# Gated feed-forward with a ternary down projection on one core: the buffers of down_w's late parts, and a new order of the first batch's steps

## The chip, the core and the metric

The kernel runs on one core of a Trainium2 chip. The core has a matrix engine (PE, with a weight-load queue PEld beside it), a vector engine (DVE), a scalar engine (ACT), a general engine (POOL) and a sync engine (SP), which issues nearly all transfers of this kernel (DMA). Each engine takes its instructions strictly in the order of the program; engines wait for each other by semaphores. The metric is the device time of one execution in microseconds (us), lower is better; several executions give a median.

## What is computed

`x` is (4, 1024, 512), `cond` is (4, 128), `norm_w` (512, 128), `up_w` (4096, 512), `down_w` (512, 2048), all float32. Cut to what matters:

```python
scale = cond @ norm_w.T + 1.0
ms = mean(x * x, axis=-1)
h = x * scale * rsqrt(ms + 1e-6)
val, gate = split(h @ up_w.T)            # 2048 columns each
h = val * gelu(gate)
hq = act_quant(h)                        # per token: round(h * 127 / max|h|), scaled back
wq = weight_quant(down_w)                # round(w / mean|w|) clipped to -1, 0, 1, scaled back
y = hq @ wq.T + x
```

## The kernel before

**Blocks and batches.** The four batches of 1024 tokens are taken one after the other. The 4096 rows of `up_w` make 16 blocks of 128 value rows and 128 gate rows; block number g is 16 times the batch plus j. A product in float32 quality is made of float16 halves: a high part and the rest ("low"). Blocks 0 to 11 of the first batch are plain products (`plain`, L715, 12 matmuls each, named `gate.j.h` and `value.j.h` for token half h). From block 12 on a block is made of seven products of six matmuls each by a Strassen-like scheme (`product`, L700): `first`, `fourth`, `second`, then `third` of the block before, `fifth`, `gate` of the block before, `value`. The sums are kept in PSUM banks A (two), B (one), E (two). Between the products stand copies and activations: ACT copies A to B (`first_copy`, L807), E out (`fourth_copy`, L815), A out (`fifth_copy`, L822) and makes the GELUs (`second_gelu`, L829, and `gate_gelu`, L846); DVE makes the outputs (`third_out` L835, `gate_sum` L843, `value_sum` L852, `value_out` L855). `second` adds into B and needs `first_copy`; `value` adds into A and needs `fifth_copy` to have read it; `third` adds into A and needs `value_sum`.

**The first batch** also has to make everything that the other batches use: it scales `up_w` by powers of two, splits and turns it (`w_*`, `rows_*`, `s_sum`, `s_high`, `s_low`, `s_turn`) and spills the parts to DRAM (`s_spill`, L469). It makes the second batch's tokens: for each quarter a of the tokens it loads, scales, sums and splits them (`t_load` to `t_low`) into a buffer with the tag `nx`, and turns that by a transposing transfer in three parts (`t_turn.a.part`, L675; part 0 holds the operands of `first` and `second`, part 1 the operand of `gate`, part 2 the rest). For a = 0 and 2 the tokens themselves stand in the tag `xn`, for a = 1 and 3 in the tag `am`; the four sums of a quarter stand in the tag `xt`. Each of these tags has one buffer. Last, it takes the running maxima (`max.i.h`, L906 and L908).

**down_w** is read twice. The first reading (`d_load`, `d_sum`) gives the mean. The second is done in eight pieces n of 128 x 1024 float32 (512 KB): `d_fetch(n)` (L546) brings a piece into a buffer, `d_round(n)` (L550, ACT) and `d_sign(n)` (L557, ACT) make it ternary in `tn`, and `d_turn(m)` (L560) turns two pieces at once into `wd`. The buffers of the pieces are those of the tokens, used again, by tag; piece 2 has a place of its own in H. A fetch waits until the last reader of its buffer is done, and holds the sync engine while it waits.

**Order.** The whole program's order is written by hand (`manual_schedule`). For the first batch it is a list of 619 steps, `FIRST_BATCH`, found by a search; a step emits its instructions for whichever engines they need. A third number 1 at a `s_sum`, `s_low` or `t_sum` puts that step on DVE, otherwise it is on POOL. The list reaches to the products of block 15. From block 16 on a loop over slots emits the products; there pieces 2 to 7 are rounded by a table (`D_LATE`: `d_round` 2 and `d_sign` 2 in the x part of slot 16, `d_round` 3 in its y part), and `d_turn` 0 and `d_fetch` 4 are issued after slot 16 between the first two loads of block 18's weights (L485, L483).

Of the kernel before, what the change touches and what calls it, by code (L numbers as in the profile page):

```python
# [51 lines left out]
def glu_quant_kernel(  # L52
# [456 lines left out]
    def d_at(n):  # L509

        return n // 4 + 2 * (n % 2), n // 2 % 2, n % 2
# [26 lines left out]
    def d_fetch(n):  # L538

        if n == 2:  # L540
            v = H[:, NJ].rearrange("p h t -> p (h t)")
        else:
            tag = ("xn", "xt", None, "nx", "xn", "xt", "nx", "xn")[n]
            v = wpool.tile([P, HF], F32, name=f"dn_{n}", tag=tag, bufs=1)
        c, u, _ = d_at(n)
        SP.dma_start(out=v, in_=down_w[c * P : (c + 1) * P, u * HF : (u + 1) * HF])  # L546
        dn[n] = v
# [701 lines left out]
    def second_part():  # L1249
# [110 lines left out]
    def take(steps):  # L1360
# [17 lines left out]
        value.3.0 rows_high.5 o_low.3 t_square.0.0 gelu.3.0 rows_low.5 rows_turn.5 o_high.2 gate.3.1 out.2.1
        gelu.3.1 c_range out.3.0 w_load.9 value.3.1 s_spill.4.1 s_sum.3.0.1 s_sum.3.2 w_load.7 w_range.6
        s_spill.3.1 w_load.11 d_load.1 t_square.0.1 s_spill.2.0 w_factor.6 c_spread o_low.2 w_scale.6.1  # L1380
        c_rows gate.4.0 w_scale.6.0 s_sum.3.1.1 s_high.2.1 rows_high.6 s_low.2.1.1 out.3.1 s_sum.3.3
        rows_low.6 rows_turn.6 s_high.3.1 value.4.0 s_high.3.0 s_low.3.0 max.0.0.0 d_sum.3 w_range.7
        max.1.0.0 gate.4.1 t_root.0 o_high.0 c_copy c_store w_factor.7 s_sum.4.1 w_load.8 w_scale.7.0
        o_low.0 gelu.4.0 value.4.1 w_scale.7.1 s_sum.4.0.1 s_sum.4.2.1 rows_high.7 out.4.0 max.1.0.1 d_sum.0
        s_low.3.1.1 gate.5.0 rows_low.7 rows_turn.7 s_high.4.0 s_low.4.0 max.0.1.0 d_sum.1 c_undo gelu.4.1
        value.5.0 out.4.1 w_range.8 c_load s_spill.3.0 s_sum.4.3 d_total s_spill.6.1 s_spill.5.1 w_factor.8
        s_high.4.1 s_low.4.1 w_scale.8.1 max.1.1.0 d_spread gate.5.1 w_scale.8.0 s_sum.5.1 s_sum.5.0.1
        rows_high.8 s_spill.7.1 s_sum.5.2.1 s_spill.2.2 rows_low.8 s_sum.5.3 s_high.5.0 value.5.1
        rows_turn.8 w_range.9 s_low.5.0.1 s_sum.6.0.1 w_factor.9 w_scale.9.0 s_sum.6.2 gate.6.0 c_bring
        w_scale.9.1 t_scale.0.1 w_gain.6 max.1.1.1 gelu.5.1 s_spill.4.0 t_sum.0.0.1 s_spill.4.2 rows_high.9  # L1390
        d_mean value.6.0 out.5.1 s_spill.3.2 s_high.5.1 t_load.1 rows_low.9 t_high.0.1 t_scale.0.0 t_sum.0.2
        w_range.10 gate.6.1 gelu.6.0 w_factor.10 w_gain.8 s_low.5.1.1 s_sum.6.3 s_sum.6.1.1 s_high.6.0
        value.6.1 rows_turn.9 t_sum.0.3.1 gelu.5.0 t_sum.0.1 s_high.6.1 s_low.6.0.1 s_sum.7.0 t_high.0.2
        out.5.0 gelu.6.1 gate.7.0 t_low.0.2 t_high.0.0 w_scale.10.1 s_sum.7.2 w_scale.10.0 s_spill.8.1
        s_sum.7.1.1 t_turn.0.2 rows_high.10 value.7.0 out.6.1 t_low.0.1 gelu.7.0 rows_low.10 s_high.7.0
        s_spill.5.0 s_low.6.1.1 gate.7.1 s_sum.7.3.1 w_range.11 t_low.0.0 t_turn.0.0 out.7.0 t_square.1.0
        w_factor.11 w_scale.11.1 s_low.7.0.1 s_sum.8.1 s_spill.5.2 value.7.1 t_turn.0.1 w_scale.11.0 out.6.0
        t_square.1.1 max.2.0.0 s_spill.6.2 gelu.7.1 t_root.1 rows_turn.10 rows_high.11 gate.8.0 s_sum.8.0.1
        s_high.7.1 s_low.7.1.1 gelu.8.0 s_sum.8.2.1 out.7.1 s_spill.7.2 s_sum.8.3 rows_low.11 s_spill.6.0
        value.8.0 s_spill.9.1 s_high.8.0 s_low.8.0.1 s_spill.8.0 s_high.8.1 gate.8.1 s_sum.9.0.1 out.8.0  # L1400
        s_sum.9.2.1 s_sum.9.1.1 s_high.9.0 s_low.9.0 s_low.8.1.1 s_spill.8.2 s_sum.9.3.1 max.2.0.1 gelu.8.1
        value.8.1 w_load.12 rows_turn.11 max.3.0.0 w_gain.10 w_range.12 t_scale.1.1 gate.9.0 out.8.1
        t_scale.1.0 t_sum.1.1 s_sum.10.0.1 gelu.9.0 t_load.2 s_spill.7.0 t_sum.1.0 t_sum.1.2.1 value.9.0
        s_spill.11.1 s_high.9.1 w_factor.12 t_sum.1.3 w_gain.12 w_scale.12.1 s_sum.10.1.1 s_sum.10.2.1
        t_high.1.2 s_low.9.1.1 s_sum.10.3 gate.9.1 out.9.0 s_spill.10.1 t_high.1.0 s_spill.9.0 s_high.10.0
        w_load.13 t_low.1.2 s_low.10.0.1 value.9.1 t_turn.1.2 s_high.10.1 w_scale.12.0 t_high.1.1
        s_sum.11.1.1 gelu.9.1 s_sum.11.0 rows_high.12 gate.10.0 t_low.1.0 t_turn.1.0 t_square.2.0
        rows_low.12 t_square.2.1 out.9.1 w_range.13 rows_turn.12 s_sum.11.2.1 value.10.0 t_low.1.1
        s_low.10.1.1 gelu.10.0 max.3.0.1 s_high.11.0 t_turn.1.1 s_sum.11.3 s_low.11.0.1 w_load.14 gate.10.1
        s_spill.12.1 t_root.2 w_factor.13 w_scale.13.1 out.10.0 s_high.11.1 s_sum.12.1 s_low.11.1.1  # L1410
        w_scale.13.0 rows_high.13 value.10.1 s_sum.12.0.1 s_sum.12.2.1 rows_low.13 s_high.12.0 s_sum.12.3.1
# [417 lines left out]
```

## Time and profile before

| what | us |
|---|---|
| median of 3 runs | 721.25 (720.65 to 723.73) |
| the profiled execution, own time | 722.66 |
| its span, first to last instruction | 720.8 |
| products of block 16 begin (first, on PE) | 176.35 |
| `d_fetch` 0 and 1 issued | 163.95, 165.82 |
| `d_fetch` 2 and 3 issued | 175.54, 183.22 |

The difference between the profiled execution's own time and its span, 1.86 us, lies outside the first and the last instruction. The page's busy shares are averages over the whole span; what a change in one stage is worth is read from that stage's rows: what each engine waited for, and for how long.

### The profile page before, as it was taken

What the parts mean: (1) busy time and instruction counts of PE and PEld (TensorE: products, weight loads), DVE (VectorE), ACT (ScalarE), POOL (GpSimd) and SP (SyncE); (2) the same over time, 40 slices, a digit from 0 to 9 for tenths busy, and PEclk for the clock granted to TensorE, in tenths of its full rate; (3) what the DMA queues carried; (4) which work ended last, traced back from release to release, by engine and by line L of the source; (5) the groups of instructions that cost most, each with busy time, mean ns of one, the idle gap of its engine ahead of it and who ended that gap; (6) DMA issues with size and microseconds to landing.
All of it is one profiled execution on the core that took longest, in us unless ns stands there. A gap on an engine that the chain in (4) does not pass through costs nothing.

```text
span 720.8 us, 10222 instructions
## 1 busy us (share of the span) xinstructions
PE 712.9 (99%) x3664; PEld 359.6 (50%) x3664; DVE 589.5 (82%) x880; ACT 423.2 (59%) x703; POOL 134.7 (19%) x143
## 2 busy tenths in 40 slices
PE   8999999999899999999999999999999999999998
PEld 4544444444344446665444445665444444445854
DVE  8898898889798879897788867876689888755896
ACT  6998877676568774554335676544433665333473
POOL 1812323240100125340100031460020000000120
PEclk9999999999999999999999999999999999999999
DMA  6899889999976566777644547775944444443253
GB/s 227 282 265 285 256 222 268 243 218 221 247 181 131 132 161 146 196 185 164 156 101 115 131 101 193 175 169 165 208 103 103 101 102 103 99 91 105 104 161 132
DMA packets 227060, 121.57 MB, mean 169 GB/s; under 512 B 188969, under 2 KB 198461, under 8 KB 227010
## 3 DMA queue, kind: packets, MB, share of 16 engines
q1 hardware_dynamic: 226858, 120.80, 67.4%
q8 instruction: 28, 0.46, 0.3%
q14 instruction: 22, 0.18, 0.1%
q10 hardware_dynamic: 152, 0.13, 0.1%
HBM read 52.71 MB, written 23.09 MB: 105 GB/s over the span
## 4 chain that ended last, share of the span: by engine, by line
PE 97%; DMA 1%; ACT 1%; issue 1%; DVE 0%; SPq 0%; DVEq 0%
PE A L700 36%; PE E L700 18%; PE po L1064 9%; PE B L700 9%; PE pg L715 8%; PE pv L715 8%; PE po_end L1016 4%; DMA R<-nx 1%; PE pz L1181 1%; PE ptx L1165 1%; PE pv L786 0%; PE po_B L1064 0%; PE pg L786 0%; PE pw L382 0%; PE po_A L1064 0%
## 5 line engine op out<-in xcount | busy, mean ns | idle before, releaser
L700 PEld LDWEIGHTS <-SXY 128*128 128x128 f16 x2100 | 205.5, 98 | 242.4 <-issue 2.0
L700 PE MATMUL A<-R,SXY 128*128 128x512 f16 x1146 | 264.8, 379 | 0.0
L700 PE MATMUL E<-R,SXY 128*128 128x512 f16 x582 | 141.4, 379 | 0.0
L835 DVE SCALAR_TENSOR_TENSOR H<-A,sg,t 128x512 f32<-128x512 f32 x52 | 38.9, 748 | 66.9 <-PE A L700 66.7
L987 DVE TENSOR_TENSOR H<-H,am 128x1024 f32<-128x1024 f32 x64 | 76.0, 1213 | 0.0
L700 PE MATMUL B<-R,SXY 128*128 128x512 f16 x300 | 72.9, 379 | 1.7 <-ACT B L807 1.7
L846 ACT ACTIVATE t<-t,sg 128x512 f32<-128x512 f32 x52 | 37.4, 720 | 61.8 <-DVE t L843 61.7
L906 DVE TENSOR_REDUCE gm<-H 128x512 f32<-128x1024 f32 x56 | 69.0, 1232 | 1.0
L922 POOL PARTITION_ALL_REDUCE am<-R x8 | 14.3, 1793 | 233.4 <-DVE R L908 233.4
L829 ACT ACTIVATE t<-B,sg 128x512 f32<-128x512 f32 x52 | 35.7, 687 | 37.2 <-PE B L700 37.1
L715 PEld LDWEIGHTS <-SXY 128*128 128x128 f16 x342 | 33.4, 98 | 40.3 <-DVE SXY L424 0.4
L822 ACT COPY t<-A 128x512 f32<-128x512 f32 x52 | 30.2, 581 | 38.0 <-PE A L700 37.5
L1064 PE MATMUL po<-wd,R 128*128 128x256 fp8e4 x416 | 52.4, 273 | 0.0
L815 ACT COPY v<-E 128x512 f32<-128x512 f32 x52 | 30.4, 586 | 32.2 <-PE E L700 30.0
L855 DVE SCALAR_TENSOR_TENSOR H<-v,sg,t 128x512 f32<-128x512 f32 x52 | 41.3, 794 | 9.7 <-ACT t L846 9.6
L1064 PEld LDWEIGHTS <-R 128*128 128x128 bf16 (+1 forms) x448 | 43.8, 98 | 8.9
L807 ACT COPY B<-A 128x512 f32<-128x512 f32 x52 | 29.7, 572 | 31.5 <-PE A L700 30.7
L852 DVE TENSOR_TENSOR v<-A,v 128x512 f32<-128x512 f32 x52 | 35.6, 685 | 9.7 <-PE A L700 8.6
L995 ACT ACTIVATE H<-H 128x1024 f32<-128x1024 f32 x38 | 39.9, 1050 | 5.2 <-DVE H L987 5.2
L908 DVE TENSOR_TENSOR R<-R,gm 128x512 f32<-128x512 f32 x56 | 40.5, 723 | 1.1
L715 PE MATMUL pg<-R,SXY 128*128 128x512 f16 x180 | 41.3, 379 | 0.0
L999 ACT ACTIVATE R<-H 128x1024 bf16<-128x1024 f32 x38 | 40.1, 1056 | 1.0
(237 smaller groups left out, 947.6 us busy)
## 6 DMA issues: line engine op xcount, KB each, us to landing
SXY<-s_dram SPq DMA_DIRECT2D x46, 256.0 KB, 3.1
H<-in_L_cond_up_w_dram SPq DMA_DIRECT2D x13, 512.0 KB, 4.3
SXY<-s_dram SPq DMA_DIRECT2D x46, 128.0 KB, 3.2
s_dram<-SXY SPq DMA_DIRECT2D x15, 384.0 KB, 5.0
xr<-in_x_dram SPq DMA_DIRECT2D x19, 256.0 KB, 2.9
out_dram<-xr SPq DMA_DIRECT2D x19, 256.0 KB, 2.5
H<-in_x_dram SPq DMA_DIRECT2D x8, 512.0 KB, 7.4
R<-in_L_cond_down_w_dram SPq DMA_DIRECT2D x8, 512.0 KB, 6.9
```

The lines of the kernel that those rows point to most:

```text
L700: PE.matmul(o, s[:, w, k, :], operand(g // NJ, c, l, k), start=start and n == 0, stop=stop and n == len(TERMS) - 1, skip_group_check=True,)
L715: PE.matmul(ps, a[k // 2][:, w, k % 2, :], XP[:, l, k, h * TOK : (h + 1) * TOK], start=n == 0, stop=n == len(terms) - 1,)
L829: ACT.activation(self.t1, self.B, AF.Gelu, scale=gain(self.g, 1))
L835: DVE.scalar_tensor_tensor(h_half(self.g, 0), self.A, gain(self.g, 0), self.t1, ALU.mult, ALU.mult)
L846: ACT.activation(self.t2, self.t2, AF.Gelu, scale=gain(self.g, 1))
L855: DVE.scalar_tensor_tensor(h_half(self.g, 1), self.v, gain(self.g, 0), self.t2, ALU.mult, ALU.mult)
L906: DVE.tensor_reduce(gm[0], v, AX.X, ALU.max, apply_absolute_value=True)
L908: return [largest, lambda: DVE.tensor_tensor(m, m, gm[0], ALU.max)]
L987: DVE.tensor_tensor(v, v, r.to_broadcast([P, 2, TOK]), ALU.mult)
L995: ACT.activation(v, v, AF.Copy, bias=MAGIC)
L999: ACT.activation(q, by_tile(v), AF.Copy, bias=-MAGIC)
L1064: PE.matmul(po, w[:, j], m, start=start and j == 0, stop=stop and j == n - 1, skip_group_check=True,)
```

## The change

Two things. First, `d_fetch` gives pieces 3 to 7 other tags: `xn` and `nx` change places, so that piece 3 takes the buffer of piece 0 (`xn`) and piece 4 the one that `t_turn` reads (`nx`). Pieces 4 to 7 follow: 6 takes that of 3, 7 that of 4.

```diff
-            tag = ("xn", "xt", None, "nx", "xn", "xt", "nx", "xn")[n]
+            tag = ("xn", "xt", None, "xn", "nx", "xt", "xn", "nx")[n]
```

Second, the 619 steps of `FIRST_BATCH` stand in another order. Both lists hold the same steps on the same blocks; a few sums move between POOL and DVE (`s_low.14.1`, `s_sum.15.3`, for instance, go to POOL, `s_low.15.0` and two of `t_sum.3` to DVE). The order of PE's instructions does not change at all. The end of the list, cut to the steps that the prediction speaks of:

```diff
-        s_high.15.0 s_low.15.0 t_low.2.1 max.4.0.0 t_high.3.2 slot.14.6 t_high.3.0 slot.12.15 s_spill.15.0
...
-        slot.15.7 d_round.1 s_spill.13.1 max.4.1.1 slot.15.4 d_fetch.2 gains s_spill.15.2 max.5.1.0
-        d_round.0 s_spill.9.2 slot.14.10 slot.15.5 slot.14.9 d_sign.0 max.5.1.1 slot.15.13 slot.14.11
-        t_high.3.1 slot.14.12 slot.15.14 d_sign.1 t_low.3.1 t_turn.3.1 slot.14.15 max.6.0.0 d_fetch.3
-        max.6.0.1 max.6.1.0 s_spill.15.1 s_spill.10.2 s_spill.14.1 max.6.1.1
+        slot.12.15 slot.14.3 slot.13.8 s_low.15.0.1 w_gain.15 t_low.3.2 s_turn.15.0 slot.14.4 slot.14.5
+        slot.13.9 d_fetch.1 slot.13.10 s_spill.15.0 max.4.0.1 d_fetch.0 slot.14.7 max.5.0.0 s_high.15.1
...
+        slot.14.9 t_turn.3.2 d_round.0 slot.15.4 d_sign.0 s_spill.9.2 max.4.1.1 d_fetch.2 slot.14.10
+        max.5.1.0 s_spill.15.2 slot.15.5 s_spill.11.2 s_spill.10.2 slot.15.3 d_fetch.3 slot.15.13 d_sign.1
+        max.5.1.1 s_spill.14.1 s_spill.13.1 slot.14.11 s_spill.15.1 max.6.0.0 slot.14.12 t_high.3.1
+        max.6.0.1 slot.14.15 slot.15.14 max.6.1.0 max.6.1.1 t_low.3.1 t_turn.3.1
```

On the sync engine, where the first two pieces are fetched (`s_rows` to `SXY` is `s_turn`, `s_dram` is written by `s_spill`, `R` from `nx` is `t_turn`: 8x128 is part 0, 16x128 part 2, 4x128 part 1). Before:

```order
L475 DMA_TRANSPOSE SXY_81<-s_rows_15_0_1674 128x8x128
L546 DMA dn_0_1710<-in_L0_cond_down_w_dram 128x1024
L675 DMA_TRANSPOSE R_78<-nx_1_0_963 128x4x128
L546 DMA dn_1_1722<-in_L0_cond_down_w_dram 128x1024
L475 DMA_TRANSPOSE SXY_81<-s_rows_15_1_1675 128x8x128
```

And now:

```order
L475 DMA_TRANSPOSE SXY_81<-s_rows_15_0_1651 128x8x128
L546 DMA dn_1_1714<-in_L0_cond_down_w_dram 128x1024
L469 DMA s_dram_84<-s_rows_15_0_1651 128x1024
L546 DMA dn_0_1724<-in_L0_cond_down_w_dram 128x1024
L475 DMA_TRANSPOSE SXY_81<-s_rows_15_1_1652 128x8x128
```

Piece 1 is fetched ahead of piece 0, and a spill of 256 KB stands between the two.

On the same engine, a little later, from the fetch of piece 2 (into H) to block 18's first load (L485). Before:

```order
L546 DMA H_79<-in_L0_cond_down_w_dram 128x1024
L469 DMA s_dram_84<-s_rows_15_1_1675 128x1024
L469 DMA s_dram_84<-R_78 128x512
L675 DMA_TRANSPOSE R_78<-nx_1_0_963 128x4x128
L546 DMA dn_3_1825<-in_L0_cond_down_w_dram 128x1024
L469 DMA s_dram_84<-SXY_81 128x1536
L469 DMA s_dram_84<-R_78 128x512
L469 DMA s_dram_84<-R_78 128x1536
L485 DMA SXY_81<-s_dram_84 128x1024
```

And now:

```order
L546 DMA H_79<-in_L0_cond_down_w_dram 128x1024
L469 DMA s_dram_84<-s_rows_15_1_1652 128x1024
L469 DMA s_dram_84<-R_78 128x512 x2
L546 DMA dn_3_1808<-in_L0_cond_down_w_dram 128x1024
L469 DMA s_dram_84<-R_78 128x1536
L469 DMA s_dram_84<-SXY_81 128x1536 x2
L675 DMA_TRANSPOSE R_78<-nx_1_0_956 128x4x128
L485 DMA SXY_81<-s_dram_84 128x1024
```

The last turn of the tokens goes from ahead of piece 3's fetch to the end of the list, and the spill of 384 KB from block 13's place in `SXY` (`s_spill.13.1`), which stood ahead of piece 2, goes behind piece 3.

On ACT, around the rounding of pieces 0 and 1 (`B_15` is written by `first_copy`, `t1_15` by `second_gelu`, `t2_15` from A by `fifth_copy`, `v_15` by `fourth_copy`; `t2_14` by `gate_gelu`). Before:

```order
L807 COPY B_15_1746<-A_15_1736 128x512
L815 COPY v_15_1759<-E_15_1751 128x512
L829 ACTIVATE t1_15_1778<-B_15_1746,sg_0_104 128x512
L550 ACTIVATE dn_1_1722<-dn_1_1722,wsc_106 128x1024
L550 ACTIVATE dn_0_1710<-dn_0_1710,wsc_106 128x1024
L822 COPY t2_15_1803<-A_15_1736 128x512
L557 ACTIVATE tn_0_1806<-dn_0_1710,unmagic_74 128x1024
L667 CAST nx_1_0_963<-xa_1_3_1494 128x256
L846 ACTIVATE t2_14_1708<-t2_14_1708,sg_0_104 128x512
L557 ACTIVATE tn_0_1806<-dn_1_1722,unmagic_74 128x1024
```

And now:

```order
L807 COPY B_15_1749<-A_15_1740 128x512
L550 ACTIVATE dn_1_1714<-dn_1_1714,wsc_106 128x1024
L829 ACTIVATE t1_15_1769<-B_15_1749,sg_0_104 128x512
L550 ACTIVATE dn_0_1724<-dn_0_1724,wsc_106 128x1024
L557 ACTIVATE tn_0_1788<-dn_0_1724,unmagic_74 128x1024
L822 COPY t2_15_1802<-A_15_1740 128x512
L815 COPY v_15_1806<-E_15_1752 128x512
L557 ACTIVATE tn_0_1788<-dn_1_1714,unmagic_74 128x1024
L846 ACTIVATE t2_14_1711<-t2_14_1711,sg_0_104 128x512
L667 CAST nx_1_0_956<-xa_1_3_1478 128x256
```

The sign of piece 0 moves ahead of `fifth_copy` of block 15, and `fourth_copy` of block 15 behind it.

More of the change, by code (lines that the diff above doesn't have):

```diff
@@ L1391, in glu_quant_kernel @@
[L1391 to L1400, printed above, removed]
@@ L1406, in glu_quant_kernel @@
[L1406 to L1410, printed above, removed]
@@ new lines, in glu_quant_kernel @@
+        value.6.1 rows_turn.9 gelu.5.0 t_high.0.2 out.5.0 gelu.6.1 t_low.0.2 gate.7.0 t_high.0.0
+        w_scale.10.1 out.6.1 w_scale.10.0 s_low.6.0.1 s_sum.7.0 s_high.5.1 s_spill.5.0 rows_high.10
+        t_turn.0.2 value.7.0 s_sum.7.1.1 s_low.5.1.1 s_sum.6.3 s_high.6.1 t_low.0.0 rows_low.10 t_turn.0.0
+        gate.7.1 gelu.7.0 w_range.11 s_sum.7.2 out.7.0 t_square.1.0 s_low.6.1.1 s_sum.7.3.1 s_high.7.0
+        value.7.1 t_low.0.1 w_factor.11 t_turn.0.1 w_scale.11.1 s_low.7.0.1 s_sum.8.1 w_scale.11.0
@@ new lines, in glu_quant_kernel @@
+        out.8.1 gate.9.0 s_sum.10.0 s_low.9.1 t_scale.1.0 t_load.2 t_scale.1.1 s_spill.7.0 w_gain.10
+        value.9.0 s_sum.10.1.1 t_high.1.0 s_spill.11.1 t_sum.1.0.1 t_sum.1.2.1 t_sum.1.3.1 w_factor.12
+        w_scale.12.1 t_sum.1.1.1 s_sum.10.2.1 s_spill.9.0 gate.9.1 t_high.1.2 t_low.1.2 s_sum.10.3 w_load.13
+        s_high.10.0 s_low.10.0 t_turn.1.2 value.9.1 gelu.9.0 w_gain.12 out.9.0 w_scale.12.0 s_sum.11.0.1
+        rows_high.12 t_low.1.0 t_turn.1.0 gelu.9.1 gate.10.0 rows_low.12 t_high.1.1 t_square.2.0 t_low.1.1
```

102 lines of the change are left out of this document (53 added, 49 removed).

## Prediction

> **What bounds the kernel now.** I read the page's first part, then the busy times by stretch, then the chain of waits, and last the timeline of the one place where they point.
>
> ```profile
> span 720.8 us, 10222 instructions
> PE 712.9 (99%) x3664; PEld 359.6 (50%) x3664; DVE 589.5 (82%) x880; ACT 423.2 (59%) x703; POOL 134.7 (19%) x143
> ...
> 0.00:25.00 25.00, 22.30 (x115) 12.39 (x116) 21.02 (x85) 17.81 (x40) 9.32 (x12) 1.00 0.76 255
> ...
> 150.00:175.00 25.00, 25.00 (x117) 11.37 (x116) 22.69 (x36) 17.82 (x32) 6.15 (x8) 1.00 1.07 218
> 175.00:200.00 25.00, 23.05 (x108) 10.27 (x106) 19.79 (x26) 14.27 (x20) 3.59 (x2) 1.00 0.96 237
> ...
> 700.00:721.00 21.00, 17.52 (x97) 9.28 (x95) 14.96 (x22) 8.84 (x9) 0.00 (x0) 0.99 0.45 157
> ```
>
> The columns after the length of a stretch are the busy times of PE, PEld, DVE, ACT and POOL, then PE's granted clock, the busy share of the transfer engines and GB/s. PE is busy for 712.9 of 720.8 us, so only 7.9 us can be won at all without taking work from PE: 2.70 in the first 25 us, 1.95 between 175 and 200, and the rest at the very end (21.00 less 17.52, of which 0.2 lies behind the span). Since the change leaves PE's instructions and their order alone, these gaps are what it can close, and new ones what it can open. The list of the first batch begins after the start-up, so of the 2.70 it can reach little; the end it cannot reach. The gap that it means is the middle one:
>
> ```profile
> 177.67 5.54 DMA R<-nx
> 183.21 0.02 issue
> 183.22 0.34 SPq L546
> ...
> 184.48 3.51 issue
> 187.99 1.15 ACT dn L550
> 189.14 0.61 ACT t L846
> 189.75 0.49 ACT B L807
> 190.24 0.04 issue
> 190.28 1.46 PE B L700 x6
> ```
>
> This is the chain of waits in order of time. The last turn of the tokens is issued at 177.67 and landed at 183.21; only then does SP issue the fetch of piece 3 (183.22), because both use the buffer `nx`; ACT, which takes its work in order, stands until the piece is there (187.99), and behind the rounding stand the GELU of block 15 and the copy that `second` of block 17 needs. The copy ends at 190.24, PE goes on at 190.28. How much PE loses there, the timeline tells:
>
> ```profile
> 173.76 1.46 PE L700 MATMUL E<-R 128*128 128x512 f16 x6
> 175.05 1.46 PE L700 MATMUL A<-wd,SXY 128*128 128x512 f16 x6
> ...
> 182.82 1.46 PE L700 MATMUL E<-R,SXY 128*128 128x512 f16 x6
> 184.53 1.46 PE L700 MATMUL A<-R 128*128 128x512 f16 x6 [0.25 <-ACT t L822]
> ...
> 190.28 1.46 PE L700 MATMUL B<-R,SXY 128*128 128x512 f16 x6 [1.71 <-ACT B L807]
> ...
> 194.16 1.46 PE L700 MATMUL E<-R 128*128 128x512 f16 x6
> ```
>
> The product `gate` of blocks 14, 15 and 16 starts at 173.76, 182.82 and 194.16. A block's rhythm is 9.06 us (182.82 - 173.76); the next takes 11.34. So **2.28 us** are lost in this block, 1.87 at `second` and 0.41 at `value` of block 16 (182.82 + 1.30 would be its start, it is 184.53 - 0.41 = 184.12). The idle times in brackets, 1.71 and 0.25, are less by about 0.16 each, since the end of a product overlaps the start of the next. The smaller wait has the same kind of cause:
>
> ```profile
> 181.63 1.15 ACT L550 ACTIVATE H<-H,wsc 128x1024 f32<-128x1024 f32 x1 [0.44 <-DMA H<-in_L_cond_down_w_dram]
> 182.86 1.15 ACT L557 ACTIVATE tn<-H,unmagic 128x1024 fp8e4<-128x1024 f32 x1
> 183.91 0.56 ACT L822 COPY t<-A 128x512 f32<-128x512 f32 x1
> ```
>
> Piece 2 lands 0.44 after ACT could have rounded it, and `fifth_copy`, behind it, comes late.
>
> **The change part by part.**
>
> *Piece 3 in the buffer of piece 0.* Its fetch now waits for `d_sign(0)`, not for the turn. In the rows below the sign of piece 0 (174.56) ended at 175.72, 7.5 us ahead of the old 183.22. So this wait goes; next in line is the transfer queue itself. On SP the fetch stands behind the fetch of piece 2 and four spills (256 + 3 x 128 KB by their shapes), with its own 512 KB that is 1664 KB; at the 218 GB/s of the stretch 150 to 175 that takes 7.8 us. The turn of part 2, ahead of all these, has landed by 177.64, when `fourth` of block 16 takes it without a wait; so piece 3 is there by 185.4. It must be there so that rounding, GELU and copy, 2.25 us from 187.99 to 190.24, end before `second` of block 17 would start without loss, 190.28 - 2.28 = 188.0: by 185.75. It makes that by 0.35 or more. Since `s_spill.13.1` (384 KB) moves from ahead of piece 2 to behind piece 3, piece 2 comes some 1.8 us earlier (384 KB at 218 GB/s), more than the 0.44 it was late. I take the whole 2.28; the bounds are 2.28 and, if piece 3 came as late as before, 0.
>
> *Piece 4 in `nx`.* Its fetch takes over the wait for the last turn, which now stands at the end of the list, behind `t_low.3.1`, DVE's last step. That step is some 3.7 us of DVE work later than before in the list, so the turn is issued near 182 instead of 177.67 and, with the 5.54 it took, landed by 187.5; the fetch of piece 4 was issued at 188.16 anyway. Cost nothing; its cover is 0.6 us, and what is behind it on SP is block 18's load (a rival below). Pieces 5 to 7 meet the same waits as before under other tags: nothing.
>
> *The rounding of pieces 0 and 1 in the new order.* Here I expect something to be given back.
>
> ```profile
> 162.56 1.30 SPq L475 DMA_TRANSPOSE SXY<-s_rows  x1
> 163.95 0.53 SPq L546 DMA_DIRECT2D dn<-in_L_cond_down_w_dram  x1
> ...
> dn<-in_L_cond_down_w_dram SPq DMA_DIRECT2D x1, 512.0 KB, 4.7
> ...
> 162.66 1.22 DVE L671 TENSOR_TENSOR nx<-xt,nx 128x1024 f16<-128x1024 f32 x1
> ...
> 172.01 2.17 ACT L550 ACTIVATE dn<-dn,wsc 128x1024 f32<-128x1024 f32 x2
> 174.10 0.57 ACT L822 COPY t<-A 128x512 f32<-128x512 f32 x1
> 174.56 1.16 ACT L557 ACTIVATE tn<-dn,unmagic 128x1024 fp8e4<-128x1024 f32 x1
> ```
>
> Before, ACT rounded both pieces (172.01), did `fifth_copy` of block 15 (174.10 to 174.67) and then the sign; `value` of block 15 started at 175.05, so there was 0.38 to spare. Now the sign of piece 0 stands ahead of that copy, and piece 0 is the second to be fetched. Its time follows from the first fetch, which goes into `xt` and waits for `t_low.3.2` (DVE, 162.66 before). In the new order 19 steps lie between `w_factor.15` and it, 12.0 us by their rows, against 17 steps and 11.8; so it starts near 162.9 and ends near 164.1, and the fetch is issued at about 164.3 (163.95 before). With the 4.7 from issue to landing piece 1 is there at 169.0; a spill of 256 KB and the 512 KB of piece 0 take 3.6 us more at 218 GB/s: piece 0 lands at 172.6. From there rounding to sign is 1.23 (181.63 to 182.86), sign to copy 1.05 (182.86 to 183.91), the copy 0.57: it ends at 175.45, and `value` of block 15 starts 0.4 us late, with some 0.05 for the signal **0.45**. From below: before, the second fetch was issued at 165.82 and both roundings ran from 172.01 on without a wait between them, so the second piece can be there by 172.0; then the copy ends at 174.85 and costs 0. From above: if the first fetch took 6.1, as that of piece 2 did, everything is 1.4 later, 1.85.
>
> ```profile
> H<-in_L_cond_down_w_dram SPq DMA_DIRECT2D x1, 512.0 KB, 6.1
> ```
>
> I take 0.45, since the queue there is as full as in the row with 4.7. The Trainium skill (DMA: Bandwidth & Descriptors, section Anatomy of one DMA — SWDGE (gpsimd) path) fits a transfer by 2.0 us and its bytes at 436 GB/s, an estimate of 3.2 us for 512 KB; the trace has 4.7 and 6.1 on SP's queue, so it does not hold in this queue. By that rule piece 0 would be in time, this term nothing, and the sum 2.28 instead of 1.83.
>
> *The rest of the list.* Steps before 150 us are moved by up to 8 us of their engine's work, but the long moves are those of steps that PE does not wait for soon. The one that comes nearest is `out.1.1`, 5.7 us of DVE work later than its 39.39: near 45.1, ending near 45.9, where `value.2.1` takes the bank at 46.36.
>
> ```profile
> 39.39 0.74 DVE L771 SCALAR_TENSOR_TENSOR H<-g,sg,pv 128x512 f32<-128x512 f32 x1
> ...
> 46.36 2.59 PE pv L715 x12
> ```
>
> PE had no idle time at all from 25 to 175 us; I put this part at 0, with 1 us as the other bound.
>
> **Sum.** -2.28 + 0.45 = -1.83 us: the profiled execution of 722.66 (span 720.8) would become 720.8. It was 1.4 above the median; 721.25 - 1.83 gives **719.4**.
>
> **The rivals.**
>
> *Block 18's weights come late, and part of the gain goes* (0.18). `s_spill.13.1` reads the lanes that L485 writes; it now stands behind piece 3. If piece 3 lands at 185.4 and two spills of 384 KB follow, 3.6 us at 218 GB/s, L485 is issued at 189.0 instead of 185.06, and L483 4.06 behind it at 193.1.
>
> ```profile
> 185.06 0.56 SPq L485 DMA_DIRECT2D SXY<-s_dram  x1
> ...
> 189.12 2.14 SPq L483 DMA_TRANSPOSE SXY<-s_dram  x1
> ...
> 198.21 1.29 PE E L700 x6
> ...
> SXY<-s_dram SPq DMA_TRANSPOSE x9, 3.5
> ```
>
> `fourth` of block 18 needs it at 198.21 - 1.83 = 196.4. With the 3.5 us from issue to landing that are the median of such loads from 120 to 230 us, or the 6.1 of the slowest fetch, it would be there at 196.6 to 199.2, a loss of 0.2 to 2.8; with the middle, 1.5, the time is 720.9. Against it: the queue then carries the same bytes as before without the pause of 3.5 us that piece 3 left in it, so landings should come earlier, not later.
>
> *The first fetch is late and the kernel slower* (0.15). SP is in order: while the fetch of piece 1 waits for `t_low.3.2`, the fetch of piece 0, `s_turn.15.1` and the turns of block 16's tokens stand behind it, and ACT with `fifth_copy` behind piece 0. Each microsecond by which `t_low.3.2` ends after 164.1 is then one at `value` of block 15; from 165.9 on the gain is used up. 3 us late gives 721.25 - 1.83 + 3 = 722.4. For it: DVE is busy for 22.69 of 25 us there, so nothing that slips is caught up. Against it: 12.0 against 11.8 us of work ahead.
>
> *Another place of the new list starves PE* (0.12): a bank let go or a weight turned a little too late, as at `out.1.1`. With 1 to 2 us the gain is about gone: 721.
>
> *The buffer does not help* (0.05): piece 3 comes as late by the queue as by the turn, and 0.45 is lost beside: 721.7.
>
> **How the numbers follow.** The forecast has 0.50, with 719.0 to 719.9 as its own range. The range that leaves 0.2 out runs from 718.4 (the whole 2.28, and 0.6 for the scatter of a median of runs that spread over 3 us) to 722.4 (the slower rival at 3 us). 0.5% is 3.6 us, about what a measurement of this kernel can tell from no change; a gain of that size would need more than the 2.28 and is given 0.02, a loss of that size needs the slower rival with over 5 us, or several, 0.06; within it 0.92.
>
> **What would show it.** Right: the fetch of piece 3 issued between 175 and 180 with no wait for R from `nx`; no idle time of PE at `second` of block 17; a rhythm of `gate` from block 15 to 16 of 9.1 to 9.3; a short wait of PE for ACT's L822 at `value` of block 15, 0.1 to 0.5. Wrong: idle time of PE at L715 before 142 us; ACT waiting for piece 0 after 174; a wait at `fourth` of block 18 for L483; or the rounding of piece 3 still starting after 186.

## The result, and the profile after

| what | before | after |
|---|---|---|
| median of 16 runs each, us | 722.54 (720.65 to 725.72) | 720.18 (719.41 to 720.96) |
| the profiled execution, own time | 722.66 | 720.43 |
| its span | 720.8 | 718.6 |
| from the start of `gate` of block 14 to that of block 16 | 20.40 | 18.13 |

The ratio of the times is 0.9966, with a 95% interval of 0.9956 to 0.9977: 0.3% faster, which lies within the half per cent that the prediction called no change, though the interval leaves 1 out. 720.18 lies 0.8 above the 719.4 of the forecast and inside its range. The runs also lie closer together: 5.1 us apart before, 1.6 after.

Busy times by stretch of the kernel after (length, then PE, PEld, DVE, ACT, POOL, the granted clock of PE, the transfer share, GB/s):

```profile
150.00:175.00 25.00, 25.00 (x118) 11.33 (x117) 21.90 (x36) 17.75 (x30) 6.18 (x9) 1.00 1.01 207
175.00:200.00 25.00, 25.00 (x118) 11.30 (x117) 21.94 (x31) 15.35 (x22) 3.59 (x2) 1.00 1.03 242
```

The stretch from 175 to 200, in which PE was busy for 23.05 of 25 us before, is full. What PE still waits for, by line, over the whole span (us in total, how often, the longest):

```profile
PE pz L1181 <- DVE eps L1111: 1.5, 1, 1.5
PE pg L786 <- ACT SXY L415: 0.3, 1, 0.3
PE pg L786 <- ACT R L1169: 0.3, 1, 0.3
PE ps L203 <- ACT R L197: 0.3, 1, 0.3
PE ptx L1165 <- ACT H L1158: 0.2, 1, 0.2
```

These are waits of the start-up. The two of the middle (`B L700 <- ACT B L807`, `A L700 <- ACT t L822`) are gone, and no other has come. The same place in the timeline, by engine, first PE (start and length in us, engine, line, operation, what it writes and reads; in brackets, where there is one, the idle time before it and what ended it):

```profile
173.87 1.46 PE L700 MATMUL E<-R 128*128 128x512 f16 x6
175.17 1.46 PE L700 MATMUL A<-wd,SXY 128*128 128x512 f16 x6
...
182.94 1.46 PE L700 MATMUL E<-R,SXY 128*128 128x512 f16 x6
184.23 1.46 PE L700 MATMUL A<-R 128*128 128x512 f16 x6
...
188.12 1.46 PE L700 MATMUL B<-R,SXY 128*128 128x512 f16 x6
...
192.00 1.46 PE L700 MATMUL E<-R 128*128 128x512 f16 x6
...
195.89 1.46 PE L700 MATMUL E<-R,SXY 128*128 128x512 f16 x6
```

`gate` of blocks 14, 15 and 16 begins at 173.87, 182.94 and 192.00: 9.07 and 9.06, where it was 9.06 and 11.34. ACT, in the same stretch:

```profile
171.54 0.69 ACT L829 ACTIVATE t<-B,sg 128x512 f32<-128x512 f32 x1 [0.96 <-PE B L700]
172.13 1.14 ACT L550 ACTIVATE dn<-dn,wsc 128x1024 f32<-128x1024 f32 x1
173.30 1.15 ACT L557 ACTIVATE tn<-dn,unmagic 128x1024 fp8e4<-128x1024 f32 x1
174.35 0.57 ACT L822 COPY t<-A 128x512 f32<-128x512 f32 x1
...
181.19 1.14 ACT L550 ACTIVATE H<-H,wsc 128x1024 f32<-128x1024 f32 x1
...
183.47 0.56 ACT L822 COPY t<-A 128x512 f32<-128x512 f32 x1
183.93 1.15 ACT L550 ACTIVATE dn<-dn,wsc 128x1024 f32<-128x1024 f32 x1
```

No rounding (L550) waits for a transfer: piece 3's follows the copy at 183.93, where before ACT stood until 187.99. And the starts of transfers on SP:

```profile
164.66 0.53 SPq L546 DMA_DIRECT2D dn<-in_L_cond_down_w_dram  x1
...
165.72 0.42 SPq L546 DMA_DIRECT2D dn<-in_L_cond_down_w_dram  x1
...
174.63 0.44 SPq L546 DMA_DIRECT2D H<-in_L_cond_down_w_dram  x1
...
176.69 0.41 SPq L546 DMA_DIRECT2D dn<-in_L_cond_down_w_dram  x1
...
182.11 1.19 SPq L675 DMA_TRANSPOSE R<-nx  x1
185.60 0.34 SPq L485 DMA_DIRECT2D SXY<-s_dram  x1
187.37 0.53 SPq L546 DMA_DIRECT2D dn<-in_L_cond_down_w_dram  x1
187.95 1.39 SPq L483 DMA_TRANSPOSE SXY<-s_dram  x1
```

The fetch of piece 3 is issued at 176.69, ahead of the last turn (182.11); before, it was issued at 183.22, 0.01 us behind that turn's landing.

### The profile page after: what moved, and what is told of

It is laid out like the page before. It is cut to its first block, busy times and chain, and to the rows that moved or that the text cites. A ratio compares the mean times of both kernels' runs of the same rounds, so it can differ in the third digit from the quotient of the medians.

```text
span 718.6 us, 10218 instructions
## 1 busy us (share of the span) xinstructions
PE 712.7 (99%) x3664; PEld 359.6 (50%) x3664; DVE 587.3 (82%) x880; ACT 423.6 (59%) x703; POOL 135.9 (19%) x143
## 4 chain that ended last, share of the span: by engine, by line
PE 99%; ACT 0%; DVE 0%; issue 0%
PE A L700 37%; PE E L700 19%; PE B L700 9%; PE po L1064 9%; PE pg L715 8%; PE pv L715 8%; PE po_end L1016 4%; PE pz L1181 1%; PE ptx L1165 1%; PE pv L786 0%; PE po_B L1064 0%; PE pg L786 0%; PE pw L382 0%; PE po_E L1064 0%; PE po_A L1064 0%; PE pc L211 0%
## 5 line engine op out<-in xcount | busy, mean ns | idle before, releaser
L700 PEld LDWEIGHTS <-SXY 128*128 128x128 f16 x2100 | 205.5, 98 | 240.5
L700 PE MATMUL A<-R,SXY 128*128 128x512 f16 x1146 | 264.8, 379 | 0.0
L700 PE MATMUL E<-R,SXY 128*128 128x512 f16 x582 | 141.5, 379 | 0.0
L700 PE MATMUL B<-R,SXY 128*128 128x512 f16 x300 | 72.9, 379 | 0.0
L822 ACT COPY t<-A 128x512 f32<-128x512 f32 x52 | 30.2, 580 | 37.5 <-PE A L700 37.1
L807 ACT COPY B<-A 128x512 f32<-128x512 f32 x52 | 29.7, 572 | 31.2 <-PE A L700 30.6
```

The source lines that it names most:

```text
L700: PE.matmul(o, s[:, w, k, :], operand(g // NJ, c, l, k), start=start and n == 0, stop=stop and n == len(TERMS) - 1, skip_group_check=True,)
```

## The experiments

The theory: the new buffer alone removes the loss of 2.28 us, because the fetch of piece 3 no longer waits for the turn; the new list is needed for at most the smaller wait. The rivals: the list brings it; the first fetches are on the edge; and, for what the forecast did not foresee, the narrower runs, either the start of the list or the exposed wait made the wide ones. Medians are of 12 runs each, ratios to the kernel before on the same chip. "Lost" is the time from the start of `gate` of block 14 to that of block 16 less the 18.13 of after.

| kernel | median (lowest to highest) | ratio (95%) | lost in its profile |
|---|---|---|---|
| e1 buffers alone | 720.51 (719.85 to 722.11) | 0.9973 (0.9958 to 0.9988) | 0 |
| e2 list alone | 726.50 (725.64 to 727.31) | 1.0047 (1.0031 to 1.0063) | 7.22 |
| e3 buffers and one spill | 720.58 (720.20 to 721.51) | 0.9965 (0.9949 to 0.9981) | 0 |
| e4 piece 0 late | 721.61 (720.99 to 722.36) | 0.9981 (0.9965 to 0.9998) | 1.34 |
| e5 piece 0 late, ACT reordered | 721.27 (720.55 to 722.21) | 0.9987 (0.9972 to 1.0001) | 0.80 |
| e6 old start, rest of after | 720.51 (719.66 to 720.79) | 0.9969 (0.9954 to 0.9985) | 0 |
| e7 new start, rest of before | 722.67 (720.73 to 724.82) | 1.0001 (0.9983 to 1.0019) | 1.01 |
| e9 two spills behind the fetch | 725.94 (724.49 to 726.55) | 1.0035 (1.0018 to 1.0052) | 5.31 |
| e12 one spill behind the fetch | 721.14 (720.32 to 724.57) | 0.9986 (0.9968 to 1.0003) | 0.77 |

**The buffers alone (e1).** The kernel before with one line changed:

```diff
-            tag = ("xn", "xt", None, "nx", "xn", "xt", "nx", "xn")[n]
+            tag = ("xn", "xt", None, "xn", "nx", "xt", "xn", "nx")[n]
```

> The order of before, word for word, with the new buffers alone (pieces 3 and 4 exchanged with nx and xn as in the change). Theory, that the buffer brings the gain: the fetch of piece 3 is issued near 179 instead of 183.22, its rounding no longer waits, and the 1.87 us of idle PE at `second` of block 17 goes; the 0.41 at `value` of block 16 stays, since piece 2 and the spill ahead of it are where they were. About 1.9 us less than before (ratio 0.997). Rival, that the new order of the list brings it: no difference (ratio 1.000) and PE idle at `second` of block 17 as before. On the spread of runs (5.1 us before, 1.6 us after): if it came from the exposed wait for the turn and the fetch behind it, the runs lie within about 2 us here too; if from another place of the old list, within about 5.

The theory's ratio came. In its profile `gate` starts at 175.48, 184.55 and 193.61, 9.07 and 9.06 apart, so even the 0.41 at `value` of block 16 was not there. (It is not in the profiles of e7, e8, e10 and e11 either, which have the old buffers: of five such executions only the prediction's shows it.) But its profiled run, 722.11, was the highest of the twelve, and PE's waits show a line that the others lack:

```profile
PE pmean L528 <- DVE wpart L523: 0.8, 1, 0.8
```

PE stood for the mean of `down_w` at 76 us, since ACT, which sums the pieces, had waited before:

```profile
58.91 0.63 ACT L322 ACTIVATE H<-H 128x512 f16<-128x512 f32 x1 [1.08 <-DMA H<-in_L_cond_up_w_dram]
```

So from there on this execution ran 1.2 us behind e3's, which has the same first part of the list (1.5 us by `gate` of block 14). Four of the twelve runs lay near 722 (721.77 to 722.11), the other eight at 719.85 to 720.69. Whether all four lost at this place is open; one has a profile.

**The list alone (e2).** The kernel after with the old buffers, and the fetch of piece 3 put last:

```diff
-            tag = ("xn", "xt", None, "xn", "nx", "xt", "xn", "nx")[n]
+            tag = ("xn", "xt", None, "nx", "xn", "xt", "nx", "xn")[n]
...
-        max.5.1.0 s_spill.15.2 slot.15.5 s_spill.11.2 s_spill.10.2 slot.15.3 d_fetch.3 slot.15.13 d_sign.1
...
-        max.6.0.1 slot.14.15 slot.15.14 max.6.1.0 max.6.1.1 t_low.3.1 t_turn.3.1
+        max.5.1.0 s_spill.15.2 slot.15.5 s_spill.11.2 s_spill.10.2 slot.15.3 slot.15.13 d_sign.1 max.5.1.1
...
+        slot.14.15 slot.15.14 max.6.1.0 max.6.1.1 t_low.3.1 t_turn.3.1 d_fetch.3
```

> The new order of the list with the old buffers; since the last turn reads the buffer xn that piece 3 takes then, the fetch of piece 3 stands last in the list, behind that turn. Theory: the turn is issued at 182.1 and landed after 186.9, the fetch follows at 187 and lands at 191.5 to 192.5, the rounding is done near 194, against 185.75 when `second` of block 17 wants it: PE idle there for 6 to 8 us, and the kernel 3.5 to 5.5 us slower than before (ratio 1.005 to 1.008). Rival, that the new order brings the gain: faster than before by 1 to 2 us, the idle time of PE elsewhere. On the spread: if an exposed wait for turn and fetch makes it, the runs lie some 5 us apart again; else within 2 as in after.

The buffer in question is `nx`: the turn reads it, and piece 3 takes it here. The median is 4.1 us over before's median of 722.36, as the theory has it: the list without the buffer loses. The 7.22 lost are not all waiting. PE's timeline there:

```profile
186.36 1.46 PE L700 MATMUL E<-R,SXY 128*128 128x512 f16 x6
192.17 2.72 PE L700 MATMUL B<-R,SXY 128*128 128x512 f16 x6 [4.35 <-ACT B L807]
194.69 2.77 PE L700 MATMUL A<-R 128*128 128x512 f16 x6
...
198.76 1.46 PE L700 MATMUL E<-R 128*128 128x512 f16 x6
```

PE waits for 4.35, shorter than expected, since the turn was landed 3.67 after its issue and the fetch went out at 185.30. Then products of the same six matmuls take 2.72 and 2.77 instead of 1.46. The granted clock (third column from the end) says why:

```profile
188.00:190.00 2.00, 0.00 (x0) 0.00 (x0) 0.00 (x0) 0.12 (x1) 0.00 (x0) 1.00 1.25 262
190.00:192.00 2.00, 0.00 (x0) 0.00 (x0) 0.33 (x1) 2.00 (x3) 0.00 (x0) 0.71 1.03 287
192.00:193.00 1.00, 0.83 (x3) 0.27 (x3) 0.96 (x2) 0.61 (x2) 0.00 (x0) 0.50 1.15 315
...
197.00:198.00 1.00, 1.00 (x5) 0.35 (x3) 0.51 (x1) 0.00 (x0) 0.00 (x0) 0.66 0.11 31
198.00:199.00 1.00, 1.00 (x7) 0.41 (x5) 0.97 (x3) 0.04 (x1) 0.00 (x0) 1.00 1.14 212
```

It falls to 0.50 within 190 to 192, during the wait, and is back at 1.00 by 198; the last 2.7 of the 7.22 us are lost to it. The wide runs did not come: 1.7 us apart, with the longest exposed wait of all. So a long wait does not by itself scatter.

**Buffers and one spill (e3).** e1 with `s_spill.13.1` moved from ahead of the fetch of piece 2 to behind that of piece 3:

```diff
-        slot.15.7 d_round.1 s_spill.13.1 max.4.1.1 slot.15.4 d_fetch.2 gains s_spill.15.2 max.5.1.0
...
-        t_high.3.1 slot.14.12 slot.15.14 d_sign.1 t_low.3.1 t_turn.3.1 slot.14.15 max.6.0.0 d_fetch.3
...
+        slot.15.7 d_round.1 max.4.1.1 slot.15.4 d_fetch.2 gains s_spill.15.2 max.5.1.0 d_round.0 s_spill.9.2
...
+        slot.15.14 d_sign.1 t_low.3.1 t_turn.3.1 slot.14.15 max.6.0.0 d_fetch.3 s_spill.13.1 max.6.0.1
```

> The order of before with the new buffers, and s_spill.13.1 moved behind the fetch of piece 3: two parts of the change and none of the rest of the new list. Theory: both idle places go, 2.28 us less than before, the same as after (ratio 0.996 to 0.9975; 0.4 us less than with the buffers alone). Rival, that the rest of the list is needed for it: as with the buffers alone, the 0.41 at `value` of block 16 remains (ratio 0.9975 to 0.998), or nothing at all is gained (1.000).

The ratio is that of after (0.9965 beside 0.9966), and nothing is lost in the middle. So the rest of the new list is not needed for this. That the spill by itself brought 0.4 over e1 is not shown: the medians stand at 720.51 and 720.58.

**Piece 0 late (e4).** After, one step moved:

```diff
-        slot.13.9 d_fetch.1 slot.13.10 s_spill.15.0 max.4.0.1 d_fetch.0 slot.14.7 max.5.0.0 s_high.15.1
-        s_low.15.1 s_turn.15.1 slot.14.13 slot.13.11 slot.15.0 slot.14.14 slot.13.12 slot.15.1 max.5.0.1
+        slot.13.9 d_fetch.1 slot.13.10 s_spill.15.0 max.4.0.1 slot.14.7 max.5.0.0 s_high.15.1 s_low.15.1
+        s_turn.15.1 d_fetch.0 slot.14.13 slot.13.11 slot.15.0 slot.14.14 slot.13.12 slot.15.1 max.5.0.1
```

> After, with the fetch of piece 0 moved behind s_turn.15.1 (a dose of what the slower rival feared: piece 0 late, with `fifth_copy` of block 15 behind its rounding on ACT). Theory: the fetch is issued near 169.2 instead of 165.7, lands 4.6 us later at 173.9, the rounding of piece 0 takes 1.15 and the copy follows, so the bank of `value` of block 15 comes 1.3 to 1.7 us late: PE idle there for about 1.5 us and the kernel 1.5 us slower than after (ratio to before 0.998 to 0.9995). Rival, that there is slack of some 2 us ahead of this bank, as the 0.45 that was forecast and not found could mean: less than 0.3 us slower than after (ratio 0.9965 to 0.9972).

1.43 over after, and ACT shows the steps that the prediction priced at 0.45:

```profile
173.46 1.15 ACT L550 ACTIVATE dn<-dn,wsc 128x1024 f32<-128x1024 f32 x1 [1.43 <-DMA dn<-in_L_cond_down_w_dram]
174.64 1.15 ACT L557 ACTIVATE tn<-dn,unmagic 128x1024 fp8e4<-128x1024 f32 x1
175.69 0.56 ACT L822 COPY t<-A 128x512 f32<-128x512 f32 x1
```

The copy ends at 176.25 instead of 174.92, and PE waits 1.18 for it. The mechanism is real; in after the piece was there in time. The fetch was issued at 169.08 instead of 165.72: 3.4 us of lateness cost 1.34, so some 2 us of it were free.

**The same, with ACT's steps moved too (e5).** `d_round.0` and `d_sign.0` go behind `slot.15.3`, the copies of block 15 first:

```diff
-        slot.14.9 t_turn.3.2 d_round.0 slot.15.4 d_sign.0 s_spill.9.2 max.4.1.1 d_fetch.2 slot.14.10
-        max.5.1.0 s_spill.15.2 slot.15.5 s_spill.11.2 s_spill.10.2 slot.15.3 d_fetch.3 slot.15.13 d_sign.1
+        slot.14.9 t_turn.3.2 slot.15.4 s_spill.9.2 max.4.1.1 d_fetch.2 slot.14.10 max.5.1.0 s_spill.15.2
+        slot.15.5 s_spill.11.2 s_spill.10.2 slot.15.3 d_round.0 d_sign.0 d_fetch.3 slot.15.13 d_sign.1
```

> The late fetch of piece 0 as in e4 (its PE wait for ACT's L822 was 1.2 us), and in addition the rounding and the sign of piece 0 moved behind the copies of block 15 on ACT (`fifth_copy` and `fourth_copy`, slots 15.4, 15.5 and 15.3). Theory, that the fetch is harmless in itself and costs only because ACT is in order and the copy stands behind the rounding: the 1.2 us goes again, and the time is that of after within 0.4 us (ratio to before 0.9962 to 0.9972). Rival, that the late bytes themselves are missed (by the turn of these weights, or by what follows them on the queue): 1 us or more stays lost (ratio about 0.998).

Neither came: 1.1 us over after. The wait at `value` of block 15 is gone, and the rounding follows the copies without a wait for the bytes. But it and the two signs, 3.4 us together, now stand ahead of the next block's copy:

```profile
174.93 0.59 ACT L815 COPY v<-E 128x512 f32<-128x512 f32 x1
175.41 1.16 ACT L550 ACTIVATE dn<-dn,wsc 128x1024 f32<-128x1024 f32 x1
176.60 2.19 ACT L557 ACTIVATE tn<-dn,unmagic 128x1024 fp8e4<-128x1024 f32 x2
...
179.60 0.58 ACT L807 COPY B<-A 128x512 f32<-128x512 f32 x1
```

and PE waits 0.64 at `second` of block 16 instead. So the lateness was passed on along ACT, not removed.

**The start and the rest of the list apart (e6, e7).** e6 is after with all steps up to `d_mean` in before's order; e7 is before, old buffers, with all steps up to `d_mean` in after's order, the reverse edit. The first lines of e6's against after's:

```diff
-        w_load.3 d_load.2 t_load.0 d_load.6 d_load.4 s_sum.0.1 o_whole.0.0.0 gate.1.0 x_scale.6 w_range.3
-        x_scale.7 gelu.1.0 o_whole.2.2.0 turn.4 w_range.2 turn.5 w_load.4 turn.6 turn.7 d_load.7 x_high.0
+        d_load.2 w_load.3 d_load.6 d_load.4 t_load.0 s_sum.0.1 o_whole.0.0.0 gate.1.0 w_range.3 x_scale.7
+        o_whole.2.2.0 x_scale.6 turn.4 w_range.2 gelu.1.0 turn.5 w_load.4 turn.6 turn.7 d_load.5 value.1.0
...
```

> The first part of the list (up to d_mean, the first 84 us) in the order of before, the rest as in after, new buffers. The question is the spread: before's runs lie 5.7 us apart, after's 1.6; the profile of the buffers alone (722.11, 1.5 over its median of 720.51) had PE waiting 0.8 us at L528 for the mean of down_w, which before's list reaches 0.2 us behind its last operand and after's 1.1 us behind. Theory, that the old start makes part of the spread: some runs 1 to 2 us above the others (a third of them, as with the buffers alone), the lowest runs as in after (719.4 to 720). Rival, that the start is nothing: all runs within 2 us and the median within 0.4 us of after's.

> The reverse: the first part of the list (up to d_mean) in the new order, the rest as in before, old buffers, so that the fetch of piece 3 still waits for the turn. Theory, that the middle's 2.28 us is a matter of the buffer, and the start a matter of the spread: PE idle for about 2.2 us between 180 and 190 as before, the lowest runs near 720.7, but no runs over 723.5 (before had 14 of 35 there); median 721.5 to 722.3. Rival, that the spread comes from the exposed wait for turn and fetch: runs over 723.5 remain, and the median is that of before within 0.4 us (ratio 1.000).

The theory of the start falls twice. With the old start no run lies above 720.79; with the new start, and the fetch of piece 3 behind the turn, the runs lie 4.1 us apart, five of them over 723.4, and the ratio is 1.0001. The searched start of the list brings nothing that these runs can tell; the runs over 723.4 go with the fetch that waits.

**The kernel before, profiled again (e8, e10, e11).** Nothing is edited; three more executions.

> The kernel before, unchanged, for one more profile. If its run falls among those over 723.4 (14 of 35), the profile shows where such a run loses: at L528 (the mean of down_w), 1 to 2 us by the theory of the start; at `second` of block 17 with 4 us or more by the theory of the exposed wait. If it falls at 720.5 to 722.6, it shows what a low run loses there, 1.5 to 2.3 us at blocks 16 and 17.

> The kernel before, unchanged, once more, for a profile. If its run falls over 723.4: the fetch of piece 3 comes 6 us or more behind the issue of the last turn and `second` of block 17 loses 3 us or more, if the exposed wait makes the spread; no more than 2.3 us there and the rest elsewhere, if not. If it falls below, the loss at block 17 and the time should go together as in the other three (0.5 us at 721.12, 1.0 at 722.07, 2.3 at 722.66).

> As the run before this one: the kernel before, unchanged, for one more profile, with the same expectations.

All three fell low: 721.12, 720.95 and 721.20. With e7 and the first profile, five executions have the wait. The starts on SP in e8, with two that come earlier:

```profile
168.85 1.47 SPq L675 DMA_TRANSPOSE R<-nx  x1
...
174.09 0.44 SPq L546 DMA_DIRECT2D H<-in_L_cond_down_w_dram  x1
...
177.87 1.20 SPq L675 DMA_TRANSPOSE R<-nx  x1
181.71 0.34 SPq L546 DMA_DIRECT2D dn<-in_L_cond_down_w_dram  x1
```

The fetch comes 3.84 behind the turn's issue; in e10 and e11 4.15 and 3.72, in e7 4.34, in the profile of the prediction 5.54. The time lost, in this order: 0.54, 0.75, 0.28, 1.01, 2.27. So the 2.28 is the value of one execution, and the other four lose less than half of it. The link between the time of a run and this wait is loose among the low ones (721.20 with 0.28 lost, 720.95 with 0.75), whose starts differ by about as much.

**Spills out of the turn's way (e9, e12).** The kernel before; e9 moves two spills of 256 KB and 128 KB by their shapes behind the fetch of piece 3 (the expectation gives both as 256), e12 only the second, `s_spill.9.2`. The edit of e9:

```diff
-        slot.15.7 d_round.1 s_spill.13.1 max.4.1.1 slot.15.4 d_fetch.2 gains s_spill.15.2 max.5.1.0
-        d_round.0 s_spill.9.2 slot.14.10 slot.15.5 slot.14.9 d_sign.0 max.5.1.1 slot.15.13 slot.14.11
-        t_high.3.1 slot.14.12 slot.15.14 d_sign.1 t_low.3.1 t_turn.3.1 slot.14.15 max.6.0.0 d_fetch.3
...
+        slot.15.7 d_round.1 s_spill.13.1 max.4.1.1 slot.15.4 d_fetch.2 gains max.5.1.0 d_round.0 slot.14.10
...
+        d_sign.1 t_low.3.1 t_turn.3.1 slot.14.15 max.6.0.0 d_fetch.3 s_spill.15.2 s_spill.9.2 max.6.0.1
```

> The kernel before with old buffers, but the two spills of 256 KB that stand on SP's queue between the fetch of piece 2 and the last turn (s_spill.15.2 and s_spill.9.2) moved behind the fetch of piece 3. The fetch still waits for the turn. In three executions with that wait the fetch was issued 3.84, 4.34 and 5.54 us behind the turn's own issue, and `second` of block 17 came 0.5, 1.0 and 2.3 us late. Theory, that the wait itself is short on an empty queue and varies with what the queue still carries: the fetch 3.2 to 4.0 us behind the turn's issue, 0 to 0.6 us lost, median 720.3 to 721.3 and no run over 723. Rival, that the turn takes its time and its scatter by itself: 4 to 5.5 us, median within 0.4 us of before's, runs over 723.4 remain.

> The kernel before with old buffers, and only s_spill.9.2 moved behind the fetch of piece 3; s_spill.15.2 stays where it was, since moving it made ACT's sign of piece 2 wait 3.87 us for the buffer that this spill reads. Theory, that the exposed wait is short when less stands on the queue ahead of the last turn, and that its scatter makes before's: the fetch of piece 3 is issued 3.2 to 4.0 us behind the turn's issue (3.23 with both spills moved, 3.72 to 5.54 in five executions with both in place), 0 to 0.5 us lost at `second` of block 17, median 720.3 to 721.3, no run over 723. Rival, that before's high runs (723.4 to 726) come from elsewhere: the profile may look so, but a third of the runs lie over 723.4 and the median is within 0.4 us of before's.

In e9 the fetch did come 3.23 behind the turn's issue (178.35, 181.58), yet the kernel lost 5.31, for another reason:

```profile
186.76 1.15 ACT L557 ACTIVATE tn<-H,unmagic 128x1024 fp8e4<-128x1024 f32 x1 [3.87 <-DMA s_dram<-s_rows]
187.82 0.56 ACT L822 COPY t<-A 128x512 f32<-128x512 f32 x1
```

The sign of piece 2 writes into the buffer that `s_spill.15.2` reads, and ACT, in order, held the copy behind it: the very kind of conflict that the change removes, made anew by moving a transfer. e12 avoids that and lost 0.77, with the fetch 4.23 behind the turn: above the 3.2 to 4.0 that the theory gave. Its median is where the theory put it, 0.8 under before's, but one run of twelve (724.57) lies over 723.4, where none should. High runs seem rarer than in before, where 41 of 114 lie over 723.4; twelve runs do not settle that.

The rows do say what the wait goes with, if it is counted from the fetch of piece 2 and not from the turn. From the issue of piece 2's fetch to that of piece 3's the five executions with both spills in between took 7.30 to 7.71 us (in before 175.54 to 183.22), e12 with 128 KB less 6.89, e9 with 384 KB less 5.84, these two from one profile each. So, as far as these seven profiles show, the turn lands when the bytes on the queue from piece 2 on have been moved, and in the five its own 3.72 to 5.54 only say how late it was issued among them. What differs between the five is when SP gets there: the issue of piece 3's fetch lies 7.63, 7.75, 8.06, 8.25 and 9.46 us behind the start of `gate` of block 14 (e11, e8, e10, e7 and the first profile), and the time lost follows it: 0.28, 0.54, 0.75, 1.01, 2.27. In the first profile SP spent 3.15 us on starting an earlier turn, in the other four 1.47 to 1.95:

```profile
168.65 3.15 SPq L675 DMA_TRANSPOSE R<-nx  x1
```

Why it took longer there is not shown.

## Why the prediction was right, and where it was off

- *PE bounds, and only the gap in the middle can be closed.* Right: the span fell by 2.2 (720.8 to 718.6), the other gaps stayed.
- *The wait for the turn goes, and the transfer queue still brings piece 3 in time: 2.28.* Right, and shown by e1 and e2: the buffer alone brings it, the list alone does not. Piece 3 was to be there by 185.4; its rounding ran at 183.93 without a wait, so it landed at least 1.5 sooner. The 218 GB/s of the stretch 150 to 175 were too low a speed here: from 177.5 to 183.5 the transfers of after moved 355 GB/s. How much of the 1.5 this makes is not shown, since no row has the landing of piece 3.
- *Piece 4 in `nx` costs nothing.* Right: the last turn was issued at 182.11 (near 182 by the forecast), the fetch of piece 4 at 187.37, 0.8 earlier than before.
- *Piece 0 comes late: 0.45 given back.* The mechanism was right (e4 shows it with 1.34), the size was not: 0. This is the term that was mis-sized. The first fetch was issued at 164.66 (forecast 164.3) and `t_low.3.2` ended at 164.41 (164.1), both a little late; but piece 0, forecast for 172.6, was rounded from 172.13 on, right behind the GELU of block 15, so 3.6 us for spill and piece behind piece 1 were too many: piece 1 landed at 169.26 (164.66 and 4.6), which leaves at most 2.9. The copy ended at 174.92, 0.25 ahead of `value` at 175.17. The lower bound, 0, was the truth. The rule weighed there (the Trainium skill, DMA: Bandwidth & Descriptors, section Anatomy of one DMA — SWDGE (gpsimd) path) also gave 0; but it is a fit for the general engine's transfers, and the estimate of 3.2 us for 512 KB is not what the runs show for SP's: the first fetch took 4.6 from issue to landing.

```profile
dn<-in_L_cond_down_w_dram SPq DMA_DIRECT2D x1, 512.0 KB, 4.6
```

- *The rest of the list: 0.* Right as far as seen: e6 has the old start and e3 the old list, with medians of 720.51 and 720.58 against 720.18; differences of 0.3 to 0.4 that intervals of some 0.15% to each side do not tell apart.
- *Block 18's weights late* (0.18): did not happen. L485 was issued at 185.60, not 189.0, L483 at 187.95, not 193.1, and `fourth` of block 18 ran at 195.89 without a wait.
- *The slower rival* (0.15): did not happen, since `t_low.3.2` ended at 164.41, 1.5 ahead of its point of 165.9. Nor was each microsecond of lateness one lost, as this rival had it: in e4 the second fetch was 3.4 late and cost 1.34.
- *The number.* 719.4 was 721.25 less 1.83. What the forecast took for the time before, the median of three runs, lay low: sixteen runs gave 722.54. The difference of the medians is 2.36, of the two profiled executions 2.23. So the whole 2.28 less nothing, from a base 1.3 higher, is how 720.18 comes about. The agreement of 2.36 with 2.28 is partly luck: the other four profiled executions with the wait lost 0.28 to 1.01, and without its five runs over 723.4 before's median would be 721.66, only 1.5 above after's.

**Before's high runs, and what stays open.** 41 of its 114 runs lie over 723.4, 5 of 12 of e7 and 1 of 12 of e12; of the 76 runs of the six kernels in which the fetch does not wait for the turn (after, e1, e3, e4, e5, e6), none is over 722.36. So they go with the wait. None of the profiles is of such a run, but the mean granted clock of nearly every run is on record. In the profile before, PE waited 1.71 in one piece and the clock stayed at 1.00; in e9 it waited 3.48, and the clock fell:

```profile
188.00:189.00 1.00, 0.56 (x2) 0.25 (x2) 0.00 (x0) 1.00 (x2) 0.00 (x0) 0.72 0.93 325
189.00:190.00 1.00, 1.00 (x4) 0.29 (x2) 0.00 (x0) 1.00 (x2) 0.00 (x0) 0.50 1.35 192
190.00:191.00 1.00, 1.00 (x4) 0.34 (x3) 0.00 (x0) 0.04 (x1) 0.00 (x0) 0.50 1.10 267
191.00:192.00 1.00, 1.00 (x4) 0.38 (x3) 0.74 (x2) 0.00 (x0) 0.00 (x0) 0.57 0.86 283
192.00:193.00 1.00, 1.00 (x7) 0.47 (x5) 0.97 (x2) 0.10 (x1) 0.00 (x0) 1.00 1.75 205
```

Those 3.4 us at half the clock cost the 1.7 us by which e9 lost more than it waited. Over the whole run they take 1.7 of some 720 us off the mean clock: it is 0.998 in this run of e9, and 0.995 in e2's, with its 6.8 us. All 24 runs of e2 and e9 have 0.995 to 0.998, none of the 76 above is below 0.999. Of before's runs 98 have a clock on record: 29 are at 0.998 or lower, and all of these lie at 723.78 or more; no run below that does. The three highest runs of e7 and the high run of e12 have 0.998 too. So most of the high runs lost time at half the clock, as e2 and e9 did, and the low ones did not, which makes two groups of before's runs. That a wait of some 3 us stood ahead of it in them is inferred. Seven of before's 36 high runs with a clock on record, at 723.45 to 724.58, have 1.000, and what made these stays open.

The Trainium skill (TensorE: Matmul & The Clock Gate, Part 1: The HAM clock gate) has PE's activity watched in free-running windows of about 3.4 us, with half the clock after an idle one; by this the phase of the window against the kernel's start differs from run to run. The half clock in e9 fits it: 0.72 in the second from 188 and 0.57 in that from 191 put its ends near 188.4 and 191.9, 3.4 apart. In e2 the clock fell near 190.8, 3.0 us after PE's last product had ended (192.17 less 4.35 is 187.82), so by these ends a little less than a whole window without products was enough there.

## What to carry to other kernels

When a fetch waits, look first at whose buffer it takes: one line, a table of tags, was worth the whole gain as far as these runs can tell, and of the reordering around it they found no part that was needed. Moving a step frees nothing unless the queue that it lands on has room and the buffer that it holds is wanted by nobody: e5 removed and e9 shortened the wait that was meant, and each made another. Take the size of a wait on a transfer from several executions: here five of the same wait cost 0.3 to 2.3 us, and removing it also narrowed the runs from 5.1 to 1.6 us. And where runs scatter, compare the mean granted clock of each: 0.998 against 1.000 told two groups apart that no profile had caught.

## What the runs showed of the hardware that was not expected

A wait of PE can cost more than its length. After 3.48 us without a product the granted clock was 0.50 for about 3.4 us, and 1.7 us were lost on top; after 4.35 it was 0.50 for about 6.8 us (from 190.8 to 197.7 by the shares 0.71 and 0.66), and 2.7 were lost. After 1.71 nothing was. One such stretch shows in the mean clock of the whole run, 0.998 where runs without it have 0.999 to 1.000, and in before it marks 29 of the 36 high runs. And the same turn of the tokens, with the same transfers ahead of it, let the fetch behind it go 3.72 to 5.54 us after its issue in five executions, while the time from the first of those transfers to that fetch was 7.30 to 7.71 us in all five.
